# Running the first element's layer 1 by itself inside a third layer 0, with a three-deep ring of score tiles, and a new order of the layers

## The chip, the cores and the metric

The kernel runs on one core of one Trainium2 chip. The metric is device time in microseconds (us) of one launch, smaller is better. The engines are named as in the profile: PE (matrix multiplication), PEld (its weight loads), DVE (vector), ACT (activation functions), POOL, and SP (the queue that issues most DMAs).

## The reference, cut to what matters

Four attention layers follow one another over a tensor of 4 elements of 64 x 64 x 64 (4096 tokens of 64 channels each). The elements are independent.

```
layer 0:  e = softmax(q k^T) over 4096 keys;  out[n] = sum over m of e[m, n] v[m];  x = gamma * out + x
layer 1:  theta = x Wt (8 channels); phi, g = maxpool2(x Wp), maxpool2(x Wg)   (1024 keys, 8 and 32 channels)
          x = x + sigma * (softmax(theta phi^T) g) Wo
layer 2:  group norm (per channel pair), attention over 4096 keys, projection, x = x + ...
layer 3:  group norm, attention over 4096 keys, projection, out = norm(x) + ...
```

Layers 0, 2 and 3 each form 4096 x 4096 scores per element. Layer 1 forms 4096 x 1024, a small part of the work.

## The kernel before

All arithmetic is in float32. A big attention (layer 0, 2 or 3 of one element) is a **stage** of 64 equal **steps**. This text writes L2/0 for the stage "layer 2 of element 0". There are twelve stages; before the change their order is L0/0, L0/1, L2/0, L0/2, L2/1, L0/3, L2/2, L3/0, L3/1, L2/3, L3/2, L3/3.

In a step, `first` makes two score tiles `s` (128 x 1024, two PSUM banks each) with four 64 x 512 matmuls apiece, and ACT writes exp of each into an SBUF tile `p`. The step also issues the second products of an earlier step (`adds` in layer 0, `then` in `attention`): they multiply `p` by the values and sum into accumulators `acc`. In layer 0 these lag three steps, and four accumulators (one bank each) stay open for the whole stage; in layers 2 and 3 they lag two steps and use two accumulators. PSUM has room for two `s` tiles (`ps_s`) and four single banks (`ps_a`); the latter are the accumulators. There are 14 `p` buffers and 13 buffers of 128 x 2048 (`x_p`).

In layers 2 and 3 the row sums are formed by DVE additions of `p` into `zacc` (L1299 in the profile). In layer 0 ACT adds them up as it writes the exponentials (`accum_out`, L1009), except where `back["at"]` is LATE or END: there ACT runs without it (L1006) and DVE reduces the tile (L1007).

Everything else is **background**: layer 1, and the preparation of later stages (`before0`, `before2`, `before3`: transposes, norms, projections, values; `loads`: the input DMA). A background is a Python generator that yields places. `step` advances it at the place MID, between the two second products of the step, and at LATE, inside the second one; an END advances after all the work of the step. `tempo` says how many advances a step earns, and at most one MID and one LATE happen in a step. `urgent` work (closing a chunk of layers 2 and 3) goes ahead of MID. `drain`, after a stage, issues all that the background has left, at once. The program order so made is the order on every engine; nothing is reordered later.

Layer 1 of an element has a prefix (theta, phi, g: L1075, L1092, DMAs that swap halves), 16 **units** (two halves j of the queries by eight blocks k of 128 keys), and `finish`. A unit is `scores` (eight matmuls with 8 rows each into two `s` tiles, L1122; two exponentials, L1128; DVE adds them to `zacc1`, L1137) and, one unit later, `add` (four 128 x 32 matmuls, L1148). For elements 1 to 3 layer 1 runs in the background of a layer 2, which needs only two accumulators, so `add` sums in a bank of its own. For element 0 it runs in the background of L0/1, where all four banks are taken: each `add` writes a fresh `s` tile, and DVE adds it to an SBUF tile (L1157).

The backgrounds before, by stage:

```
L0/0: rest of element 0's preparation, constants, loads(1), before0(1), loads(2)
L0/1: layer 1 of 0, before2(0)          L2/0: layer 1 of 1, before0(2)
L0/2: before2(1), loads(3)              L2/1: layer 1 of 2, before0(3)
L0/3: before2(2)                        L2/2: layer 1 of 3, before3(0)
L3/0: before3(1)    L3/1: before2(3)    L2/3: before3(2)    L3/2: before3(3)    L3/3: -
```

Where a layer 2 follows a layer 0, `not_before` holds the second products of layer 2 back until layer 0's accumulators are released, so that the fourth step of that layer 2 has two steps' worth of them.

Of the kernel before, what the change touches and what calls it, by code (L numbers as in the profile page):

```python
# [11 lines left out]
ALU = mybir.AluOpType  # L12
# [585 lines left out]
def fast_path(tc: tile.TileContext, a: dict, out: bass.AP, bad, read_flag):  # L598
# [18 lines left out]
    D8, D2 = C // 8, C // 2  # L617


    MID, ALONE, LATE, END = range(4)  # L620

    ctx = ExitStack()
    ctx.enter_context(tc.manual_schedule())
# [158 lines left out]
    def background(tempo, *phases):  # L782
# [5 lines left out]
        back.update(gen=pieces(), credit=0.0, tempo=tempo)  # L788
        back["at"] = next(back["gen"], None)

    def drain():
        while back["at"] is not None:
            while urgent:
                urgent.pop(0)[1]()
            back["at"] = next(back["gen"], None)
# [20 lines left out]
    def step(first=None):  # L816
        back["credit"] = min(back["credit"] + back["tempo"], 3.0)
        for f in before.pop(now[0], ()):
            f()
        if first is not None:  # L820
            first()
        work = due.pop(now[0], [])
        for n, f in enumerate(work[:2]):
            if n == 1:
                advance(MID)
            split = n == 1 and ready(LATE)
            f(lambda: advance(LATE)) if split else f()
        for f in work[2:]:
            f()
        if len(work) < 2:  # L830
            advance(MID)
            advance(LATE)
        passes = list(later)
        later.clear()
        for f in passes:
            f()
        advance(END)
        now[0] += 1

    def until(st, *names):  # L840
# [134 lines left out]
            for _ in g:  # L975
                pass

    def layer0(st):

        q, k, v = st.pop("q"), st["x"], st.pop("v")
        pairs = NB * NC // 2
        acc, ps, zs, scaled = {}, {}, {}, {}
        zsum, rz = check_columns(NB)

        def queries(m, i, e):

            c, n = divmod(m // 2, 4)
            return q[(c + i) % 2][half(i), ds(c // 2 * 1024 + m % 2 * 512 + n * P + e * C, C)]  # L990

        def first(u):
            m, c = divmod(u, NC)
            if c == 0:
                zs[m] = small.tile([P, NC], FP, tag="z0", name="z0")
            s = s_tile()
            for i in range(2):
                for e in range(2):
                    nc.tensor.matmul(  # L999
                        s[half(e), chunk(i)], queries(m, i, e), k[half(i), chunk(c)], start=True, stop=True  # L1000
                    )
            p = ps[u] = p_tile()
            z = zs[m][:, c : c + 1]
            if back["at"] in (LATE, END):

                nc.scalar.activation(p, s, AF.Exp)  # L1006
                nc.vector.tensor_reduce(z, p, AX.X, ALU.add)  # L1007
            else:
                nc.scalar.activation(p, s, AF.Exp, accum_out=z)  # L1009
            if c == NC - 1:  # L1010
                nc.vector.tensor_reduce(zsum[:, m : m + 1], zs.pop(m), AX.X, ALU.add)  # L1011
                nc.vector.reciprocal(rz[:, m : m + 1], zsum[:, m : m + 1])

        def scale(t):
            m = 2 * t // NC
            vs = scaled[t] = z_p.tile([P, C], FP, tag="vs", name="vs", bufs=1)
            nc.scalar.activation(vs, v[:, m, :], AF.Copy, scale=rz[:, m : m + 1])  # L1017

        def add(t, e, n, cols):

            m, second = divmod(2 * t, NC)
            c = (second + 2 * e) % NC + n
            if c not in acc:
                acc[c] = acc_tile()
            for i in range(2):
                nc.tensor.matmul(  # L1028
                    acc[c][half(i), cols], scaled[t][half(e), :], ps[NC * m + c][half(e), chunk(i)][:, cols],
                    start=(m == 0 and not second), stop=(m == NB - 1 and second > 0),  # L1030
                )
                yield

        def adds(t, n, within=None):
            for cols in parts(within, t * 2 < NC or t >= pairs - NC // 2):
                for row_tiles in zip(add(t, 0, n, cols), add(t, 1, n, cols)):
                    pass
            if n == 1:
                del scaled[t]
                if t % 2:  # L1040
                    for u in range(2 * t - 2, 2 * t + 2):
                        ps.pop(u)

        def finish(cs):
            xT = st["x"]
            for c in cs:
                nc.vector.scalar_tensor_tensor(xT[:, chunk(c)], acc.pop(c), gamma0, xT[:, chunk(c)], ALU.mult, ALU.add)
            if not acc:
                st["done0"] = True

        start = now[0]
        for t in range(pairs):
            g = start + t + 3
            before.setdefault(g, []).append(lambda t=t: scale(t))
            due.setdefault(g, []).extend([lambda *within, t=t, n=n: adds(t, n, *within) for n in range(2)])
        due[start + pairs + 2].append(lambda: finish((0, 2, 1, 3)))
        for t in range(pairs):
            step(lambda: (first(2 * t), first(2 * t + 1)))
        return start + pairs + 3


    def layer1(on, st, bank):

# [44 lines left out]
        yield from [MID] * 3  # L1110

        ps, accs, zaccs, os = {}, {}, {}, {}

        def scores(j, k):

            ss = [s_tile() for e in range(2)]
            n, d = divmod(k, 2)
            for m in range(2):
                for e in range(2):
                    for i in range(2):  # L1120
                        r = slice((2 * e + i) * 32, (2 * e + i) * 32 + D8)
                        nc.tensor.matmul(  # L1122
                            ss[e][half(m), chunk(i)], pgs[0 if e == d else 1][r, ds(n * P + m * C, C)],
                            th[r, chunk(i ^ j)], start=True, stop=True,
                        )
            ps[j, k] = pk = [p_tile() for e in range(2)]
            for e in range(2):
                nc.scalar.activation(pk[e], ss[e], AF.Exp)  # L1128
            if k == 0:
                return lambda: None  # L1130
            if k == 1:
# [7 lines left out]
            return accumulate  # L1139

        def add(j, k):
            if k == (NK - 1 if bank else 0):
                os[j] = o_tile("o1")
            if k == 0 and bank:
                accs[j] = acc_tile()
            acc = accs[j] if bank else s_tile()[:, 0:512]
            for q in range(4):
                nc.tensor.matmul(  # L1148
                    acc[quarter(q), :], g[:, k, :], ps[j, k][q // 2][:, chunk(q % 2)],
                    start=(k == 0 or not bank), stop=(k == NK - 1 or not bank),  # L1150
                )
            if k > 0:
                del ps[j, k]
            if k == 1:
                del ps[j, 0]
            if not bank and k > 0:
                nc.vector.tensor_tensor(os[j], os[j], acc, ALU.add)  # L1157
            elif not bank or k == NK - 1:
                nc.scalar.copy(os[j], acc)

        def normalise(j):

# [40 lines left out]

        todo = [(j, k) for j in range(2) for k in range(NK)]
        for n in range(len(todo) + 1):
            accumulate = None
            if n < len(todo):
                yield LATE
                accumulate = scores(*todo[n])
            if n:  # L1210
                if not bank:
                    yield END
                elif n == len(todo):
                    yield LATE
                add(*todo[n - 1])
            if accumulate and bank:
                later.append(accumulate)
            elif accumulate:
                accumulate()
        if bank:  # L1220
            for j in range(2):
                yield from finish(j)
        else:
            ends = [finish(j) for j in range(2)]
            at = [next(end) for end in ends]
            while at[0] is not None:
                if at[0] == ALONE:
                    yield ALONE
                    at[0] = next(ends[0], None)
                yield at[1]  # L1230
                at = [at[0] if at[0] != at[1] else next(ends[0], None), next(ends[1], None)]
        st["done1"] = True


# [538 lines left out]
    background(1.0, rest(st0), second_half(s0, s0["v"]), pause(6), constants(), loads(s1), pause(6), before0("DVE", s1), loads(s2))  # L1773
    layer0(s0)
    drain()
    background(3.0, layer1("DVE", s0, False), before2("DVE", s0))
    free = layer0(s1)
    drain()
    background(3.0, layer1("ACT", s1, True), before0("ACT", s2))
    free = layer2(s0, free)  # L1780
    drain()
    background(1.0, before2("DVE", s1), loads(s3))
    free = layer0(s2)
    drain()
    background(3.0, layer1("ACT", s2, True), before0("ACT", s3))
    free = layer2(s1, free)
    drain()
    background(1.0, before2("DVE", s2))
    free = layer0(s3)
    drain()  # L1790
    background(3.0, layer1("ACT", s3, True), before3("ACT", s0))
    free = layer2(s2, free)
    drain()
    background(0.6, before3("ACT", s1))
    free = layer3(s0, free)
    drain()
    background(0.6, before2("ACT", s3))
    free = layer3(s1, free)
# [88 lines left out]
```

## Time and profile before

| | |
|---|---|
| median of 3 runs | 2928.45 us (2926.47 to 2929.64) |
| time of the profiled execution | 2926.57 us |
| its span, first to last instruction | 2924.8 us |
| PE busy | 2893.5 us, 99% |
| DVE busy | 1871.4 us, 64% |
| ACT busy | 1799.6 us, 62% |
| granted TensorE clock, mean | 0.998 |

The rows of the profile name a line of the kernel, an engine, an operation and its tiles (out<-in). Each matmul of the program appears as two MATMUL records, so eight records of 64 x 512 are four matmuls. A busy PE is not a PE at its peak: matmuls are pipelined on parts of the array, and a step that waits a little between its matmuls still shows as busy.

### The profile page before, as it was taken

Reading aid. Unit: us, or ns where it says so; the run is one execution under the profiler, and the core shown is the slowest. Engines: PE = TensorE matmul, PEld = TensorE weight load, DVE = VectorE, ACT = ScalarE, POOL = GpSimd, SP = SyncE. Lnnn points to the kernel's source line nnn. Section 1 sums busy time; section 2 is a strip of 40 time slices with the busy share of each in tenths; the row PEclk is TensorE's granted clock in tenths of the full one; section 3 lists DMA queues with packets and bytes.
Section 4 is the critical chain, followed back from the end, with each engine's and each line's share of the span. In section 5 each row is a group of like instructions: output and inputs, shape, how many; then the busy total and the mean of one; then the engine's idle time right before and its main releaser. Section 6 shows DMA issues by size and latency. Waiting matters only on the chain.

```text
span 2924.8 us, 66545 instructions
## 1 busy us (share of the span) xinstructions
PE 2893.5 (99%) x29397; PEld 1130.5 (39%) x29397; DVE 1871.4 (64%) x2141; ACT 1799.6 (62%) x2481; POOL 33.7 (1%) x33
## 2 busy tenths in 40 slices
PE   9999999999999999999999999999999999999998
PEld 3333233333444433344443343444344444443333
DVE  2111753589821078963027898888888877878878
ACT  5666666665566766566766655555555555555554
POOL 0000000000000000000000000000000000000000
PEclk9999999999999999999999999999999999999999
DMA  2010000000001000000000000000000000000000
GB/s 38 1 30 7 1 1 16 7 5 5 20 5 30 1 7 5 5 23 16 1 1 7 5 9 20 19 5 9 5 19 8 20 5 7 6 20 5 8 5 10
DMA packets 85993, 30.64 MB, mean 10 GB/s; under 512 B 79680, under 2 KB 83776, under 8 KB 84288
## 3 DMA queue, kind: packets, MB, share of 16 engines
q1 hardware_dynamic: 83440, 25.90, 4.8%
q8 instruction: 232, 3.80, 0.6%
q10 hardware_dynamic: 2256, 0.41, 0.1%
q14 instruction: 65, 0.53, 0.1%
HBM read 4.79 MB, written 4.19 MB: 3 GB/s over the span
## 4 chain that ended last, share of the span: by engine, by line
PE 97%; DVE 1%; ACT 1%; issue 0%; DVEq 0%
PE acc L1323 30%; PE s L1288 30%; PE s L999 15%; PE acc L1028 15%; PE s L1122 2%; PE acc L1148 2%; ACT p L1128 1%; DVE zacc L1299 1%; PE s L1148 1%; PE s L891 0%; PE s L1419 0%; PE s L912 0%; PE s L1467 0%; PE s L1194 0%; PE s L1092 0%
## 5 line engine op out<-in xcount | busy, mean ns | idle before, releaser
L1293 ACT ACTIVATE p<-s 128x1024 f32<-128x1024 f32 x1024 | 994.5, 1022 | 694.8 <-PE s L1288 675.1
L1299 DVE TENSOR_TENSOR zacc<-zacc,p 128x1024 f32<-128x1024 f32 x960 | 1174.1, 1223 | 179.7 <-ACT p L1293 114.7
L1323 PE MATMUL acc<-p,v 64*64 64x512 f32 (+1 forms) x8576 | 1007.7, 572 | 0.0
L1009 ACT ACTIVATE p<-s 128x1024 f32<-128x1024 f32 x480 | 486.9, 1020 | 114.8 <-PE s L999 114.7
L1323 PEld LDWEIGHTS acc<-p,v 64*64 64x64 f32 x8576 | 348.7, 133 | 536.7 <-issue 536.7
L1028 PE MATMUL acc<-p,vs 64*64 64x512 f32 (+1 forms) x4224 | 501.4, 577 | 0.0
L1288 PE MATMUL s<-q,k 64*64 64x512 f32 x2048 | 491.5, 590 | 2.1 <-ACT p L1128 2.1
L1288 PE MATMUL s<-q,xT 64*64 64x512 f32 x2048 | 491.3, 590 | 0.0
L999 PE MATMUL s<-xT,q 64*64 64x512 f32 x2048 | 487.3, 591 | 2.4 <-DVE mean L1355 0.7
L999 PE MATMUL s<-xT,q_swapped 64*64 64x512 f32 x2048 | 487.7, 591 | 0.3 <-DVE o L1157 0.3
L1288 PE MATMUL s<-q,h_swapped 64*64 64x512 f32 x2048 | 480.7, 590 | 3.9 <-DVE v L916 3.5
L1288 PE MATMUL s<-q,k_swapped 64*64 64x512 f32 x2048 | 480.4, 590 | 0.0
L1011 DVE TENSOR_REDUCE all_z<-z 128x1 f32<-128x4 f32 x128 | 20.1, 157 | 606.4 <-ACT p L1009 602.7
L1028 PEld LDWEIGHTS acc<-p,vs 64*64 64x64 f32 x4224 | 173.5, 133 | 265.8 <-issue 264.0
L1288 PEld LDWEIGHTS s<-q,h_swapped 64*64 64x64 f32 x2048 | 149.5, 133 | 140.2 <-issue 127.2
L1288 PEld LDWEIGHTS s<-q,xT 64*64 64x64 f32 x2048 | 149.9, 133 | 133.2 <-issue 127.0
L1288 PEld LDWEIGHTS s<-q,k_swapped 64*64 64x64 f32 x2048 | 148.1, 133 | 137.5 <-issue 87.1
L999 PEld LDWEIGHTS s<-xT,q_swapped 64*64 64x64 f32 x2048 | 146.4, 133 | 141.7 <-issue 110.2
L999 PEld LDWEIGHTS s<-xT,q 64*64 64x64 f32 x2048 | 144.3, 133 | 139.2 <-issue 110.8
L1288 PEld LDWEIGHTS s<-q,k 64*64 64x64 f32 x2048 | 148.6, 133 | 116.6 <-issue 96.2
L1017 ACT ACTIVATE vs<-v,all_r 128x64 f32<-128x64 f32 x256 | 89.1, 348 | 157.7 <-PE acc L1028 80.5
L1128 ACT ACTIVATE p<-s 128x1024 f32<-128x1024 f32 x128 | 124.1, 1021 | 82.4 <-PE s L1122 78.5
(212 smaller groups left out, 1318.5 us busy)
## 6 DMA issues: line engine op xcount, KB each, us to landing
k_swapped<-k SPq DMA_DIRECT2D x8, 512.0 KB, 5.4
residual<-turned SPq DMA_DIRECT2D x128, 32.0 KB, 1.8
h_swapped<-xT SPq DMA_DIRECT2D x8, 512.0 KB, 5.3
out_dram<-turned SPq DMA_DIRECT2D x60, 64.0 KB, 2.0
xin<-in_x_dram SPq DMA_DIRECT2D x12, 256.0 KB, 6.4
q_swapped<-q SPq DMA_DIRECT2D x6, 512.0 KB, 5.3
pg<-pg SPq DMA_DIRECT2D x8, 128.0 KB, 2.3
xin<-in_x_dram SPq DMA_DIRECT2D x12, 64.0 KB, 2.3
```

The lines of the kernel that those rows point to most:

```text
L999: nc.tensor.matmul(s[half(e), chunk(i)], queries(m, i, e), k[half(i), chunk(c)], start=True, stop=True)
L1009: nc.scalar.activation(p, s, AF.Exp, accum_out=z)
L1011: nc.vector.tensor_reduce(zsum[:, m : m + 1], zs.pop(m), AX.X, ALU.add)
L1017: nc.scalar.activation(vs, v[:, m, :], AF.Copy, scale=rz[:, m : m + 1])
L1028: nc.tensor.matmul(acc[c][half(i), cols], scaled[t][half(e), :], ps[NC * m + c][half(e), chunk(i)][:, cols], start=(m == 0 and not second) ...
L1122: nc.tensor.matmul(ss[e][half(m), chunk(i)], pgs[0 if e == d else 1][r, ds(n * P + m * C, C)], th[r, chunk(i ^ j)], start=True, stop=True,)
L1128: nc.scalar.activation(pk[e], ss[e], AF.Exp)
L1148: nc.tensor.matmul(acc[quarter(q), :], g[:, k, :], ps[j, k][q // 2][:, chunk(q % 2)], start=(k == 0 or not bank), stop=(k == NK - 1 or not ...
L1288: nc.tensor.matmul(s[half(e), chunk(i)], k[(j + i) % 2][half(i), ds(j // 2 * P + e * C, C)], q[half(i), chunk(c)], start=True, stop=True,)
L1293: nc.scalar.activation(p, s, AF.Exp)
L1299: add = lambda: nc.vector.tensor_tensor(zaccs[c], p0, p, ALU.add)
L1323: nc.tensor.matmul(accs[c][e][half(i), cols], v[half(e), j, :], p[half(e), chunk(i)][:, cols], start=(j == 0), stop=(j == NB - 1),)
```

## The change

- The order of the stages becomes L0/0, L0/1, L0/2, L2/0, L0/3, L2/1, L3/0, L2/2, L3/1, L2/3, L3/2, L3/3.
- Element 0's layer 1 is made with `held=True`. Its prefix runs in the background of L0/1, after `before0` of element 2. It then yields HOLD, where `drain` stops. L0/2 is called with `hold=release`: at its fourth step, before that step's own matmuls, `release` runs all 16 units in one go with nothing between them. At that moment L0/1's four accumulators are released and L0/2 has opened none, so two banks of `ps_a` serve as a third score tile (`slots[2]`), and the other two as the accumulators of the two halves. `slot` hands out two `s` tiles and the pair of banks in turn. An exponential out of the pair of banks is two instructions of 512 columns. After the units, `finish` and `before2` run in the background of L0/2.
- Layer 1's other form, that sums in an SBUF tile, goes, and END with it; `adds` of layer 1 in layer 2 stand at the same places as before.
- Layer 0's exponentials always use `accum_out`.
- The backgrounds move with the stages:

```
L0/1: before0(2), prefix of layer 1 of 0            L0/2: 16 units alone; finish of layer 1 of 0, before2(0)
L2/0: loads(3), layer 1 of 1, before0(3)            L0/3: before2(1)
L2/1: layer 1 of 2, before3(0)                      L3/0: before2(2)
L2/2: layer 1 of 3, before3(1)                      L3/1: before2(3)
L2/3: before3(2)     L3/2: before3(3)     L3/3: -
```

The diff, cut:

```
+    def release():
+        assert back["at"] == HOLD
+        back["at"] = next(back["gen"])
+
     def drain():
-        while back["at"] is not None:
+        while back["at"] not in (None, HOLD):
...
@@ layer0
-            if back["at"] in (LATE, END):
-                nc.scalar.activation(p, s, AF.Exp)
-                nc.vector.tensor_reduce(z, p, AX.X, ALU.add)
-            else:
-                nc.scalar.activation(p, s, AF.Exp, accum_out=z)
+            nc.scalar.activation(p, s, AF.Exp, accum_out=z)
...
         start = now[0]
+        if hold is not None:
+            before.setdefault(start + 3, []).append(hold)
...
@@ layer1
+        slots = [None, None, None]
+        if held:
+            yield HOLD
+            slots[2] = [acc_tile() for i in range(2)]
+        turns = [0]
+
+        def slot():
+            if held:
+                turns[0] += 1
+            own = slots[turns[0] % 3]
+            s = None if own else s_tile()
+            return own or [s[:, chunk(i)] for i in range(2)], s
...
-            ss = [s_tile() for e in range(2)]
+            ss = [slot() for e in range(2)]
...
-                nc.scalar.activation(pk[e], ss[e], AF.Exp)
+                banks, s = ss[e]
+                for dst, src in [(pk[e], s)] if s is not None else [(pk[e][:, chunk(i)], banks[i]) for i in range(2)]:
+                    nc.scalar.activation(dst, src, AF.Exp)
...
         for n in range(len(todo) + 1):
-            accumulate = None
-            if n < len(todo):
+            if not held:
                 yield LATE
-                accumulate = scores(*todo[n])
+            accumulate = scores(*todo[n]) if n < len(todo) else None
             if n:
-                if not bank:
-                    yield END
-                elif n == len(todo):
-                    yield LATE
                 add(*todo[n - 1])
-            if accumulate and bank:
-                later.append(accumulate)
-            elif accumulate:
-                accumulate()
+            if accumulate:
+                accumulate() if held else later.append(accumulate)
...
-    background(3.0, layer1("DVE", s0, False), before2("DVE", s0))
+    background(1.0, rest(before0("DVE", s2)), layer1("DVE", s0, held=True), before2("DVE", s0))
     free = layer0(s1)
     drain()
-    background(3.0, layer1("ACT", s1, True), before0("ACT", s2))
+    back["tempo"] = 3.0
+    free = layer0(s2, hold=release)
+    drain()
+    background(3.0, loads(s3), layer1("ACT", s1), before0("ACT", s3))
     free = layer2(s0, free)
...
```

## The prediction

> **What bounds the kernel now.** I read the page first, then the busy time of each stage, then the timeline inside the stages that cost most.
>
> ```profile
> span 2924.8 us, 66545 instructions
> PE 2893.5 (99%) x29397; PEld 1130.5 (39%) x29397; DVE 1871.4 (64%) x2141; ACT 1799.6 (62%) x2481; POOL 33.7 (1%) x33
> ...
> PE 97%; DVE 1%; ACT 1%; issue 0%; DVEq 0%
> ```
>
> The chain that ended last runs through PE for 97% of the span. So a change gains only by giving PE fewer matmuls or by making it wait less. Matmuls stay the same in number, so the waits decide, and the page hides them: a stretched step counts as busy.
>
> They show in the length of a step, from one step's first exponential to the next one's on ACT. In the timeline an undisturbed step takes 3.43 us everywhere, 64 of them 219.6 us. What a stage takes beyond that is its background and its waits. The windows of four stages (length first, then busy time by engine, the granted clock, DMA):
>
> ```profile
> 248.26:528.17 279.91, 270.38 (x2804) 92.56 (x2800) 133.38 (x198) 185.51 (x323) 5.43 (x1) 1.00 0.03 7
> 796.91:1022.36 225.45, 224.72 (x2220) 95.25 (x2216) 38.48 (x106) 157.72 (x320) 5.43 (x1) 1.00 0.07 12
> 1516.54:1785.53 268.99, 268.22 (x2888) 100.05 (x2880) 227.19 (x223) 163.96 (x174) 1.46 (x1) 1.00 0.04 10
> 1785.53:2015.18 229.65, 226.17 (x2260) 95.08 (x2264) 187.34 (x183) 131.12 (x138) 1.46 (x1) 0.99 0.05 11
> ```
>
> These are L0/1, L0/2, L2/2 and L3/0; over 219.6 they have 60.3, 5.8, 49.4 and 10.0 us. L0/1, the stage the change takes apart, is the dearest of all twelve. Its units run from the step at 285.49 to the one at 396.37: 18 steps in 110.88 us, that is 49.1 above 18 x 3.43. One of these steps in the timeline (start, duration):
>
> ```profile
> 303.97 1.94 ACT L1006 ACTIVATE p<-s 128x1024 f32<-128x1024 f32 x2 [1.06 <-PE s L999]
> ...
> 304.60 1.47 PE L1028 MATMUL acc<-p,vs 64*64 64x512 f32 x16
> ...
> 306.00 1.11 PE L1122 MATMUL s<-th,pg 8*64 8x512 f32 x16
> 307.05 0.66 PE L1028 MATMUL acc<-p,vs 64*64 64x256 f32 x8
> 307.19 1.94 ACT L1128 ACTIVATE p<-s 128x1024 f32<-128x1024 f32 x2 [1.28 <-PE s L1122]
> ...
> 308.27 1.06 PE L1148 MATMUL s<-p,pg 128*32 128x512 f32 x8 [0.56 <-ACT p L1128]
> ```
>
> It takes 6.45 us, 3.02 more than a plain step, though its unit holds only 2.04 us of PE work (scores 306.00 to 307.05; add 308.27 to 309.26, where the next stage matmul starts). The other microsecond is the ring of two score tiles: scores wait for the stage's exponentials, the add needs a score tile as well and waits for the unit's first exponential, the next `first` waits for the second and for DVE.
>
> The chip also loses a visible piece at the start of L3/0. In the waits of PE:
>
> ```profile
> PE s L1288 <- DVE v L916: 3.5, 1, 3.5
> ```
>
> This is `drain` at the end of L2/2: both value tiles of before3(0) are issued in the last step, both score tiles wait for DVE (whose queue holds two 1.27 us additions and a 1.25 us transpose), and L3/0's first step takes 8.60 us.
>
> **The units alone (L0/2, fourth step).** Count from T, when PE could go on with the stage. Ready: at the same seam between L0/0 and L0/1 the last second products start at 255.74, T is 257.46, and DVE's four updates (L1047, 2.73 us together) start at 256.85. So the first two of the four banks are free at T + 0.8; in the built order these are the two that become the third tile. The first unit's scores end at T + 1.9, its first exponential starts at T + 2.0.
>
> Period: in the built order of the changed kernel the first tile of unit n needs the exponential 2n-3, the second the exponential 2n-2. So one exponential of the pair is always under way while PE works. From the end of exponential 2n-2: scores after 0.09 (305.91 to 306.00), the next exponential 1.19 after them (306.00 to 307.19), and 1.02 for itself: 2.30 us. In the 1.28 of that ACT does the pair's other exponential (0.92 when back to back, half of 1.94). Five of the 16 first tiles are the pair of banks, two exponentials of 512: the nearest row, L1159's copy of 512, takes 585 ns against L878's 1016 for 1024, so 1.08 to 1.17 instead of 1.02; I take 1.08. Fifteen periods: 15 x 2.30 + 5 x 0.06 = 34.8, and 0.2 for the one ACT copy between the halves. DVE needs 14 x 2.35 = 32.9 (303.55 in the timeline: two additions in 2.35), PE 16 x 2.04 = 32.6: both just under it, and `p` buffers are reused only four units later. So the last pair starts at T + 37.0, ends 2.0 later, the last add takes 0.9 more: **39.9 us** for what now costs 49.1. Bounds: PE alone, 2.0 + 32.6 + 1.9 = 36.5; both exponentials waited for, a period of 1.28 + 1.94 = 3.22, 2.0 + 15 x 3.22 + 2.9 = 53.2. The value is nearest to the first, since the built order shows which exponential is waited for.
>
> Behind this block wait: on PE the rest of L0/2 (that is the 39.9), on ACT the next `vs` scaling, on DVE layer 0's sums of 0.16 us. The six `p` tiles of steps one to three are ready when it ends. SP issues nothing in it.
>
> **The rest of layer 1 and before2(0).** `finish` cost 2.7 in L0/1 (both halves interleaved); apart, as in L2/0, two L1194 of 0.86 and two sums of 0.3: 2.3. The prefix (2.9) and before2(0) (5.5) only change stage. Layer 0's sums on ACT again (198 ns each, 32 of them) lie in ACT's idle time: a plain step there uses 2.6 of 3.43.
>
> **Moved backgrounds.** I price each stage by the one that has the same work now, in us above 219.6:
>
> - L0/1: 60.3 now. Then before0(2) 3.8 (in L2/0, the five steps from 741.24) and the prefix 2.9: 6.7.
> - L0/2: 5.8 now. Then 39.9 + 2.3 + 5.5 = 47.7.
> - The three layers 2 with a layer 1: 49.1, 49.1, 49.4 now. Then before0 sits in one and before3 in two: 49.1 + 49.4 + 49.4, less 1.7, since L2/2 now follows a layer 3 and has no step with doubled second products (5.15 us at 538.47): 146.2 after 147.6.
> - L0/3: 5.8 both times (before2).
> - L3/0: 10.0 now. Then before2, as in L3/1 now (6.8), and 0.3 for the end of a layer 2 before it: 7.1.
> - L3/1: 6.8 now, then 7.1. The others keep their work.
>
> The stall of 5.2 is inside the 10.0. It goes because these layers 1 no longer wait for their layer 0 to end: in the built order before3(0)'s value tiles come in the 60th and 61st step of L2/1 instead of both in the last. Those of before3(1) come in the last two steps of L2/2, one each, as the 53rd and 54th of L2/0 have them now at 0.97 a piece. loads(3) goes ahead of layer 1's DMAs on SP, in L2/0's first step; the first wait for those is six steps later.
>
> Sum: before 60.3 + 5.8 + 147.6 + 5.8 + 10.0 + 6.8 = 236.3; after 6.7 + 47.7 + 146.2 + 5.8 + 7.1 + 7.1 = 220.6: **15.7 us less**. The profiled execution took 2926.57, so 2910.9. The median of before is 1.9 higher; by it, 2912.8. I say 2912.
>
> **A rule against it.** The windows of the granted clock: 1.00 from 285.49 to 396.37, though PE shows 9.2 us of idle time in these 110.88; but
>
> ```profile
> 1784.00:1791.00 7.00, 3.46 (x63) 1.37 (x57) 5.94 (x6) 1.02 (x1) 0.00 (x0) 0.82 0.01 2
> ```
>
> around the 3.5 us stall, after which 64 x 512 matmuls take 1.12 us instead of 0.59. So the clock falls after a long wait, and short ones, 0.4 to 0.6 apiece, left it alone. The new block's waits are of the short kind, about 0.3 us per unit and 0.9 at its ends, so I price no loss.
>
> [...]
>
> **The rivals.**
>
> 1. *The third tile does not decouple* (same). Each unit waits for both its exponentials: the block takes 53.2, the gain is 2.4, 2926. For it: scores of both tiles are interleaved, so the first cannot finish alone. Against: the waits in the built order.
> 2. *The clock falls in the block* (slower). At the 1.06 us that those slowed matmuls settle at, for 0.59, a unit needs 2.04 x 1.80 = 3.67 on PE, the block 2.0 + 58.7 + 2.9 = 63.6: 8.0 us slower, 2936. It decides from a block of 55.6 us, 3.4 a unit. Against: 1.00 in the units of now.
> 3. *The stall only moves* to L3/1: 5.2 back, 2917. For: value tiles still stand in L2/2's last two steps. Against: one a step, and DVE's additions of that step are issued after it.
>
> That the change does not do what it says is excluded by the built order: the 16 units stand alone, with the banks as every third tile.
>
> **How the numbers follow.** Forecast 0.78; third tile 0.08; clock 0.06; moved stall 0.08. Range: down by 3.4 (block at 36.5), 2 for the median against one execution and 2.6 for stages priced by another's row: 2904. Up by the moved stall and by a block midway to rival 1 with the same 2: about 2922. Left out: rivals 1 and 2 and a little, under 2 in 10. A measurement can tell about 0.2%, 5.9 us. Faster 0.86, same 0.08, slower 0.06.
>
> **What would show it.** L0/2 of about 267 us, L0/1 of 226; in the block exponentials about 2.3 us a unit, clock 1.00; L3/0's first step 3.43; no wait of PE for L916's line over 1 us. A block over 46 us, or another stage 3 us off its price, makes the prediction wrong.

## The result, and the profile after

| | before (same chip) | after |
|---|---|---|
| median | 2926.51 us (2924.86 to 2929.64) | 2937.46 us (2936.71 to 2938.21) |
| span of the profiled execution | 2924.8 us | 2935.6 us |
| granted clock, mean | 0.998 | 0.989 |

The ratio is 1.0035 [1.0024, 1.0046]: the changed kernel is slower, by about 11 us. The prediction said 2912 and 2904 to 2922; it was wrong, on the other side of no change.

From the page of the changed kernel: span, busy time by engine, the granted clock in 40 slices, and the shares of the chain that ended last.

```profile
span 2935.6 us, 66287 instructions
...
PE 2913.2 (99%) x29269; PEld 1132.9 (39%) x29269; DVE 1826.2 (62%) x2095; ACT 1805.5 (62%) x2524; POOL 33.8 (1%) x33
...
PEclk9999998799999999999999999999999999999999
...
PE 96%; DVE 3%; issue 1%; ACT 0%; DMA 0%; DVEq 0%; ACTq 0%
```

PE is busy for 19.7 us more than before although it has 128 fewer matmul records. That is the first sign that matmuls became slower and not that waits were added. The second is the clock row: an 8 and a 7 in the slices from 440 to 587 us, which lie in L0/2.

The stages of the changed kernel, cut as in the prediction (length, then busy time by engine, granted clock, DMA). These are L0/1, L0/2, L2/0, L2/1, L3/0 and L2/2:

```profile
247.62:473.83 226.21, 226.21 (x2228) 81.46 (x2224) 24.79 (x78) 157.95 (x320) 0.00 (x0) 1.00 0.04 8
473.83:763.05 289.22, 288.24 (x2644) 98.21 (x2640) 85.16 (x148) 190.65 (x365) 5.43 (x1) 0.90 0.06 9
763.05:1033.94 270.89, 268.58 (x2876) 104.49 (x2872) 225.89 (x210) 161.87 (x170) 0.00 (x0) 1.00 0.04 10
1259.39:1530.23 270.84, 269.01 (x2892) 102.52 (x2888) 228.94 (x224) 164.18 (x175) 1.46 (x1) 1.00 0.04 10
1530.23:1757.06 226.83, 226.59 (x2260) 97.32 (x2256) 195.30 (x194) 128.69 (x135) 5.44 (x1) 1.00 0.05 11
1757.06:2025.49 268.43, 267.19 (x2884) 97.00 (x2880) 231.70 (x230) 163.89 (x174) 1.46 (x1) 1.00 0.05 11
```

| stage | priced | measured |
|---|---|---|
| L0/1 | 226.3 | 226.2 |
| L0/2 | 267.3 | 289.2 |
| three layers 2 with a layer 1, above 3 x 219.6 | 146.2 | 151.4 |
| L3/0 (first step 3.43 both) | 226.7 | 226.8 |
| L3/1 | 226.7 | 226.8 |

Two rows are off. L0/2 has 21.9 us too much, the three layers 2 have 5.2. With the 15.7 that was priced as gain, 21.9 + 5.2 - 15.7 = 11.4, and the span grew by 10.8.

In L0/2 all of it is in the block: the step that holds the 16 units takes 65.25 us, so the block is 65.25 - 3.43 = 61.8 against 39.9 priced. Windows of the changed kernel in and around the block:

```profile
476.00:485.00 9.00, 9.00 (x88) 2.92 (x80) 2.90 (x6) 4.93 (x10) 0.00 (x0) 1.00 0.01 2
485.00:486.00 1.00, 0.12 (x2) 0.00 (x0) 0.15 (x1) 0.98 (x2) 0.00 (x0) 1.00 0.00 0
486.00:487.00 1.00, 0.90 (x6) 0.32 (x12) 0.00 (x0) 1.00 (x3) 0.00 (x0) 0.57 0.00 0
495.00:505.00 10.00, 10.00 (x64) 1.27 (x56) 5.60 (x6) 5.50 (x8) 0.00 (x0) 0.50 0.01 2
545.00:555.00 10.00, 10.00 (x96) 3.52 (x93) 2.71 (x5) 7.79 (x16) 0.00 (x0) 1.00 0.00 0
```

The first unit's scores run at 1.00. At 486.13 the granted clock goes to 0.50, and it stays there until 544.16, while the block's last two adds follow one another (from 541.32); the stage's own matmuls start only at 544.80. In the window from 495 the profile has PE busy for all of its 10.00 us: this is no stall, it is work at half speed. ACT, which should have been near its limit, is busy for 5.50. A unit in the timeline (start, duration):

```profile
495.64 1.94 PE L1160 MATMUL acc<-p,pg 128*32 128x512 f32 x8
495.79 1.02 ACT L1143 ACTIVATE p<-s 128x1024 f32<-128x1024 f32 x1 [1.82 <-PE acc L1135]
496.71 1.08 ACT L1143 ACTIVATE p<-acc 128x512 f32<-128x512 f32 x2
497.51 2.01 PE L1135 MATMUL s<-th,pg 8*64 8x512 f32 x16
499.45 1.94 PE L1160 MATMUL acc<-p,pg 128*32 128x512 f32 x8
499.59 1.94 ACT L1143 ACTIVATE p<-s 128x1024 f32<-128x1024 f32 x2 [1.81 <-PE s L1135]
```

Scores take 2.01 us where the rows of before had 1.11, the add 1.94 where they had 1.06; the period is 3.80 us (495.79 to 499.59), PE's alone, and ACT waits 1.8 us for PE in each. The two exponentials of 512 take 1.08 together, as priced.

### The profile page after: what moved, and what is told of

It is laid out like the page before. It is cut to its first block, busy times and chain, and to the rows that moved or that the text cites. A ratio compares the mean times of both kernels' runs of the same rounds, so it can differ in the third digit from the quotient of the medians.

```text
span 2935.6 us, 66287 instructions
## 1 busy us (share of the span) xinstructions
PE 2913.2 (99%) x29269; PEld 1132.9 (39%) x29269; DVE 1826.2 (62%) x2095; ACT 1805.5 (62%) x2524; POOL 33.8 (1%) x33
## 4 chain that ended last, share of the span: by engine, by line
PE 96%; DVE 3%; issue 1%; ACT 0%; DMA 0%; DVEq 0%; ACTq 0%
PE acc L1317 29%; PE s L1282 29%; PE s L1002 15%; PE acc L1026 15%; PE acc L1160 3%; PE s L1135 2%; DVE zacc L1293 2%; PE s L915 0%; PE s L894 0%; PE s L1413 0%; PE acc L1135 0%; ACT p L1143 0%; PE s L1092 0%; PE s L1205 0%; PE s L1461 0%
## 5 line engine op out<-in xcount | busy, mean ns | idle before, releaser
L1287 ACT ACTIVATE p<-s 128x1024 f32<-128x1024 f32 x1024 | 994.9, 1022 | 693.7 <-PE s L1282 668.2
L1007 ACT ACTIVATE p<-s 128x1024 f32<-128x1024 f32 x512 | 519.7, 1020 | 118.3 <-PE s L1002 118.2
L1026 PE MATMUL acc<-p,vs 64*64 64x512 f32 x4096 | 496.7, 590 | 0.0
L1026 PEld LDWEIGHTS acc<-p,vs 64*64 64x64 f32 x4096 | 165.0, 133 | 260.5 <-issue 259.1
L1143 ACT ACTIVATE p<-s 128x1024 f32<-128x1024 f32 x117 | 114.1, 1022 | 81.4 <-PE s L1135 69.4
```

The source lines that it names most:

```text
L1026: nc.tensor.matmul(acc[c][half(i), cols], scaled[t][half(e), :], ps[NC * m + c][half(e), chunk(i)][:, cols], start=(m == 0 and not second) ...
L1143: nc.scalar.activation(dst, src, AF.Exp)
```

## The experiments

Four theories stood against each other. *Rows*: the clock falls because the scores read 8 of the 32 rows of each of the four groups of `theta`. *Pauses*: it falls because PE is idle for a moment in every unit. After the first four runs came *onset*, that only the first 3 us or the first wait of the block decide, and *latch*, that a fallen clock stays down until the stage's matmuls return. What is left at the end is called *share* here: the clock goes by how much of the array is at work over some microseconds. It is a reading of mine that the outcomes fit; no run shows it by itself. `r` is the slice of rows that a score matmul reads; the rows after the first 8 of each group of `theta` are zeros, so that a wider slice adds nothing to the sums.

### All 32 rows in the block

```
-  r = slice((2*e+i)*32, (2*e+i)*32 + D8)
+  r = slice((2*e+i)*32, (2*e+i)*32 + (32 if held else D8))
```

> The score matmuls of the 16 units in the block take 32 rows instead of 8; the 24 added rows of theta are zeros, so the sums stay and no instruction is added. In the changed kernel the block takes 61.8 us at a granted clock of 0.50. Theory 'rows' (the clock falls because too few rows of the array work in the scores, 8 of each 32, although PE is never idle): clock 1.00 in the block, block about 40 us, time 21 to 22 us below the changed kernel, that is 10 to 12 below the kernel before. Rival 'pauses' (the clock falls because PE waits a little in every unit): nothing changes, block 61.8 at 0.50. Rival 'seam' (the two waits of 0.9 and 1.0 us at the block's start drop the clock, and what follows only cannot raise it): the clock falls for some us at the start, and whether 32 rows raise it again is open: a block of 40 to 62.

Measured: 2914.47 us (2913.97 to 2914.85), ratio to before 0.9957 [0.9943, 0.9971]. Its window over most of the block, and two rows of its timeline:

```profile
483.00:521.00 38.00, 36.90 (x385) 9.31 (x382) 32.73 (x31) 32.14 (x44) 0.00 (x0) 1.00 0.01 2
```

```profile
499.55 1.29 PE L1135 MATMUL s<-th,pg 32*64 32x512 f32 x16
500.77 1.07 PE L1160 MATMUL acc<-p,pg 128*32 128x512 f32 x8
```

The clock is 1.00, and the add, which was not edited, is back at 1.07. The block's step takes 42.34 us, the block 38.9 (39.9 were priced), L0/2 266.3. So the 23 us between this kernel and the changed one are the clock's, and multiplying zeros brings them back. What makes the clock fall is not settled by it: the rows were changed, but with the speed the waits changed too.

### The same with two score tiles

```
-  own = slots[turns[0] % 3]
+  own = None                       (and the 32 rows)
```

> As e1_rows32, but without the pair of banks as a third score tile: the units use the two score tiles alone. If the clock stays at 1.00, each unit waits for both exponentials of the one before, 3.22 us a unit, and the block takes about 53 us instead of 40: 13 us slower than e1_rows32. If the third tile decouples nothing, the same time as e1_rows32. If the clock falls here, about 62 or more.

Measured: 2927.25 us, ratio 1.000 [0.9991, 1.001]; the block is 51.7 us at clock 1.00. Two exponentials of its timeline:

```profile
499.69 1.94 ACT L1143 ACTIVATE p<-s 128x1024 f32<-128x1024 f32 x2 [1.27 <-PE s L1135]
502.84 1.94 ACT L1143 ACTIVATE p<-s 128x1024 f32<-128x1024 f32 x2 [1.21 <-PE s L1135]
```

A unit takes 3.15 us: 1.94 for both exponentials and 1.21 of waiting for PE, which itself waits for both. The third tile is worth 51.7 - 38.9 = 12.8 us; the prediction's two prices, 53.2 and 39.9, differ by 13.3. Also, the whole gain over before hangs on the third tile.

### The 8-row scores twice, and once with 32 and once with 8 rows

```
-  for m in range(2): ...
+  for rr in ([D8, D8] if held else [D8]):         first kernel
+  for rr in ([32, D8] if held else [D8]):         second kernel
+      for m in range(2): ...                      (slice of rr rows; the second pass writes the same sums again)
```

> The changed kernel with each score matmul of the block issued twice in a row into the same place (8 rows, the second overwrites the first with the same values). At full clock a unit then needs about 3.0 us of PE, more than ACT and DVE, so that PE does not pause in the block. 'Pauses': the clock stays at 1.00 and the block takes about 52 us, 10 less than in the changed kernel although it has more work. 'Rows': the clock falls to 0.50 all the same, a unit needs about 5.9 us and the block about 97. 'Seam': as 'rows'.

> The counterpart of e3_twice8 with as many instructions: each score matmul of the block is issued with 32 rows and then with 8 into the same place, the sums being the same. Theory 'share' (the gate weighs how much of the array works, over some three microseconds, and rows that take no part count as idle; PE's pauses matter only as a part of that): clock 1.00 all through, about 3.0 us a unit on PE, block about 50 instead of e3_twice8's 87. Rival: it is the doubled matmuls, or 8 rows wherever they stand, that drop the clock: 0.50 and 85 or more.

Measured: 2963.34 us (one run) and 2927.82 us (one run). The instructions are the same in number, order and shape of output; only the rows of half the scores differ. The windows of the first and of the second:

```profile
491.00:565.00 74.00, 74.00 (x540) 14.61 (x544) 30.55 (x26) 27.05 (x37) 0.00 (x0) 0.50 0.00 1
```

```profile
484.00:530.00 46.00, 44.98 (x589) 16.85 (x577) 29.40 (x26) 28.92 (x40) 0.00 (x0) 1.00 0.01 2
```

In the first the profile has no idle moment of PE in 74 us, and the granted clock is 0.50. So no pauses are needed to keep the clock down, and *pauses* falls as the reason for the 0.50 in the units. In the second PE does pause, for 1.02 us in the block's opening, and the clock is 1.00. The opening of the first has the same wait, 1.03 us, and its clock falls at 488.92, 1.4 us after it: that few rows alone, without a pause, would make the clock fall is not shown. Blocks: 87.5 us (97 was expected by *rows*) and 52.6 us (50). The "three microseconds" over which *share* was to count is an estimate that no run shows; in the changed kernel 2.99 us lie between the block's first scores (483.14) and the fall (486.13).

### 32 rows in the first six units only

```
+  ... + (32 if held and (j, k) < (0, 6) else D8)
```

> The changed kernel with 32 rows in the scores of the first six units only, 8 rows in the other ten. 'Rows': clock 1.00 in the first six units (2.3 us each), 0.50 some us after them (3.8 us each): the block about 55. 'Seam': if 32 rows carry the block over its start, the clock stays at 1.00 to the end, block about 40. 'Pauses': 0.50 from the start, block 61.8.

Measured: 2915.62 us (one run), block 38.9, as with 32 rows throughout. The window of the six units, then that of the ten with 8 rows:

```profile
484.00:498.00 14.00, 13.02 (x143) 3.36 (x142) 10.84 (x12) 10.82 (x15) 0.00 (x0) 1.00 0.01 1
498.00:521.00 23.00, 22.88 (x242) 5.79 (x244) 20.89 (x20) 20.62 (x29) 0.00 (x0) 1.00 0.01 2
```

Ten 8-row units in 23 us leave the clock at 1.00. So *rows* falls in its plain form, that 8-row units cannot hold the clock. Here they held it, at full speed already. It also shows that 32 rows cost no more time here than 8: the block's step is 42.34 us in both, and a score matmul record takes 613 ns in the mean in both, first with 32 rows throughout (486 to 521), then with 8 in the ten units:

```profile
L1135 PE MATMUL s<-th,pg 32*64 32x512 f32 x156 | 18.6, 613 | 1.0 <-ACT p L1143 1.0
```

```profile
L1135 PE MATMUL s<-th,pg 8*64 8x512 f32 x104 | 12.7, 613 | 0.0
```

### 32 rows in the first unit only, and no first wait

```
+  ... + (32 if held and (j, k) == (0, 0) else D8)      first kernel
-  turns = [0]                                          second kernel (8 rows)
+  turns = [-1]
```

With `turns` at -1 the first unit takes two `s` tiles and the second unit starts on the free pair of banks, so the wait of 1.0 us before the second unit's scores goes.

> The changed kernel with 32 rows in the scores of the first unit only, 8 rows in the other fifteen. Theory 'onset' (the clock is dropped by the first three microseconds of the block alone, which hold 8-row scores and two waits and no add yet; later units, each with a full add, keep a full clock but cannot win it back): clock 1.00, block 39 as in e1_rows32, 23 us below the changed kernel. Theory 'rows' in a weaker form (several units of 8 rows have to follow one another early): the clock falls after the first unit, block 55 to 60.

> The changed kernel with 8 rows throughout, but the two score tiles handed out first and the pair of banks third (turns from -1): the first unit does not wait 0.4 to 0.9 us for layer 0's last updates on DVE. One of the block's two opening waits is gone, the other, for the first exponential, stays at about 1 us or grows to 1.3. If the clock needs both waits to fall, it stays at 1.00 and the block takes about 38. If the 8-row scores with one wait are enough, it falls to 0.50 and the block takes about 61.

Measured: 2936.61 and 2936.46 us (one run each), blocks of 60.5 and 61.1. The window of the first in which its clock falls:

```profile
486.00:489.40 3.40, 2.56 (x28) 0.89 (x36) 0.34 (x1) 3.17 (x5) 0.00 (x0) 0.96 0.00 0
490.00:540.00 50.00, 50.00 (x326) 6.92 (x312) 29.46 (x26) 26.25 (x36) 0.00 (x0) 0.50 0.01 1
```

With 32 rows in the first unit the fall comes one unit later, at 489.15 for 486.13, and the clock stays down. Without the first wait, of which 0.33 us are left, it comes at 486.81. Neither the first 3 us nor the first wait decides alone; *onset* falls in that form.

### 16 rows throughout, and 32 rows from the seventh unit

```
+  ... + (16 if held else D8)                            first kernel
+  ... + (32 if held and (j, k) >= (0, 6) else D8)       second kernel
```

> The changed kernel with 16 rows in all scores of the block, between the 8 that lose the clock and the 32 that keep it. 'Share': 16 rows give the opening about half of what 32 give it, and the outcome is open: if the clock holds, the block takes 39 and the kernel some 22 us less than the changed one; if it falls, the steady units, with more of the array at work than in the changed kernel, may win it back after some units: 39 to 62.

> The changed kernel with 8 rows in the first six units and 32 in the other ten. The clock falls at the start as in the changed kernel, and a unit takes 3.8 us. 'Share': with 32 rows PE uses nearly all it can at half clock, so the clock comes back within a few us of the seventh unit and the rest takes 2.3 us a unit: block about 48. 'Latch' (once down, only the stage's own matmuls bring it back): 0.50 to the end, block about 62.

Measured: 2935.46 us with 16 rows (one run), block 60.3: the clock falls and does not come back.

```profile
490.00:540.00 50.00, 50.00 (x328) 6.95 (x312) 29.06 (x26) 26.25 (x36) 0.00 (x0) 0.50 0.01 1
```

With 32 rows from the seventh unit: 2922.75 us (one run), block 47.2. Its windows from just before the first 32-row scores, which start at 504.78:

```profile
504.00:507.00 3.00, 3.00 (x24) 0.53 (x24) 2.36 (x2) 1.24 (x3) 0.00 (x0) 0.50 0.00 0
507.00:510.00 3.00, 3.00 (x32) 0.39 (x24) 2.08 (x2) 2.57 (x4) 0.00 (x0) 0.91 0.00 0
510.00:522.00 12.00, 12.00 (x134) 3.29 (x136) 9.69 (x10) 10.96 (x16) 0.00 (x0) 1.00 0.01 2
```

The clock is back at 507.56, 2.8 us after the first 32-row scores, in the middle of the block and with PE as busy as before it (3.00 of 3.00 us). *Latch* falls: with the rows given, and nothing else changed, the clock came back. A return within a few microseconds, while PE's busy share stays the same, is what *share* asks for.

### The new order without the block

Layer 1 of element 0 in its old form, in the background of L0/2, with the change's order of stages.

```
-  background(1.0, rest(before0("DVE", s2)), layer1("DVE", s0, held=True), before2("DVE", s0))
+  background(1.0, rest(before0("DVE", s2)))
...
-  free = layer0(s2, hold=release)
+  background(3.0, layer1("DVE", s0, False), before2("DVE", s0))
+  free = layer0(s2)
```

> The new order of the stages alone: element 0's layer 1 in its old form (sums in SBUF through score tiles, units between the second products), in the background of L0/2 with before2(0), and before0(2) in L0/1. By the prediction's table the order is worth 15.7 - 9.2 - 0.4 = 6 us. By the stages measured in the changed kernel (the three layers 2 with a layer 1 at 151.2 over 219.6 instead of 146.2) it is worth 1 us: no difference from before. L0/2 about 280 us, L3/0 about 227 without a long first step.

Measured: 2925.56 us (2924.09 to 2927.29), ratio 0.9996 [0.9987, 1.0005]: no change that can be told. L3/0 is 226.82, so the stall is gone as priced; L2/0 and L2/1 take 270.78 and 270.89, so they have the excess of the changed kernel too. It belongs to the order, not to the clock.

### A later start for two backgrounds

```
-  background(3.0, loads(s3), layer1("ACT", s1), before0("ACT", s3))
+  background(3.0, loads(s3), pause(2), layer1("ACT", s1), before0("ACT", s3))
...
-  background(3.0, layer1("ACT", s2), before3("ACT", s0))
+  background(3.0, pause(3), layer1("ACT", s2), before3("ACT", s0))      (and the 32 rows)
```

> e1_rows32 with layer 1 of elements 1 and 2 started two and three steps later in their layer 2 (pause(2), pause(3)), so that the sums of finish no longer fall on the step after the closing of a chunk of that layer 2 (steps 40 and 41, or 39 to 41, of the changed kernel). If that collision is what makes L2/0 and L2/1 270.8 us instead of the 269 they were priced at, L2/0 and L2/1 come down by 1.5 to 2 us each and the kernel is 3 to 4 us faster than e1_rows32, about 0.6% faster than before. If not, the same as e1_rows32.

Measured: 2912.11 us (2910.58 to 2912.35), ratio 0.9946 [0.9933, 0.996]. L2/0 is 269.08 and L2/1 270.07, against 270.84 and 270.81 with 32 rows alone. 1.8 and 0.7 us come back of the 5.2; 3 to 4 were expected. The meeting described below is gone with the shift: PE's wait for L1467, 2.2 us with 32 rows alone, is no longer among its waits, and the steps 39 to 41 come down by 2.0 us in L2/0 and by 1.7 in L2/1. In L2/1 other steps take 1.0 of that back.

### All together

32 rows, both later starts, and `turns = [-1]`.

> e8_rows32_pause with the two score tiles handed out first and the pair of banks third (turns from -1), so that the block's first unit does not wait for layer 0's last updates. With 32 rows in all units the clock stays at 1.00; the block is 0.5 to 1 us shorter than e8_rows32_pause's 38.9, and the kernel 0.5 us faster than it: some 15 us below the kernel before and 25 below the changed one.

Measured: 2911.93 us (2911.67 to 2912.29), ratio to before 0.995 [0.9936, 0.9963]; block 38.2. It is the same as the one before it within the runs' scatter, and it beats the kernel before by 0.5% and the changed one by 0.9%.

## Why the prediction was wrong, point by point

**The step that failed** is the one under "A rule against it": "The new block's waits are of the short kind, about 0.3 us per unit and 0.9 at its ends, so I price no loss." I read the clock by PE's idle time. The twice-8 kernel shows no idle time in 74 us of its block and runs at 0.50 there. In the L0/1 of before the same 8-row units stood among the stage's 64-row matmuls, and its clock of 1.00 spoke for that mixture, not for the units alone. Taking the units out of the mixture is what the change does, so this row could not speak for the block. By *share*, what was to be counted is how much of the array works in a few microseconds; an estimate of it stands below.

**The second rival** is what happened, and its price held: block 63.6 priced, 61.8 measured; 2936 priced, 2937.46 measured. It decided from 3.4 us a unit; 3.8 were seen. Its chance of 0.06 was the mistake, not its sum, though that the total comes so near is partly luck: the block was 1.8 us shorter than priced there, and the three layers 2, which it did not doubt, 5.2 us longer.

**The third tile** decouples as said: 38.9 us at full clock for 39.9 priced, 12.8 us less than with two tiles for 13.3. The first rival falls.

**The stall** of L2/2's end went and did not come again: L3/0's first step is 3.43, L3/1 within 0.1 us of its price. The third rival falls.

**The moved backgrounds** were right for L0/1, L3/0 and L3/1 and mis-sized for the layers 2: 146.2 priced, 151.4 measured (51.3, 51.2 and 48.8). I priced each by the stage with the same work and did not ask at which step two pieces would meet. The waits of PE in the changed kernel name such a meeting in L2/0 and L2/1:

```profile
PE s L1282 <- DVE xT L1467: 2.3, 2, 1.6
```

L1467 is DVE's last operation in closing a chunk of layer 2. It reads an `s` tile, and `finish`'s sums (L1187) take the other one for DVE a step later. In L2/0 the 41st step is 5.53 us long, and in L2/1 the 39th to 41st take 3.71, 4.44 and 4.42 instead of 3.43. The 1.1 us of L2/2, and what the shifted starts left in L2/1, are not traced to a cause. So the order alone, priced at 6.1 us (15.7 less the block's 9.2 and `finish`'s 0.4), brought 1.7 by medians of the same chip (2927.26 to 2925.56), which the interval given above does not tell from nothing, and most of the rest was given back in these stages.

**The sum corrected.** The order 1.7 us faster, the block with its third tile at full clock 11 faster (2914.47 for 2925.56), the clock 23 slower (2937.46 for 2914.47): with these three, taken on chips whose runs of the kernel before agree within 1 us, one comes out at 10 us slower. They divide the difference that was measured and are no check of it. The forecast's 2912 was meant for a kernel that keeps its clock: with that alone restored, by the 32 rows, the time is 2914.47. The 2911.93 of the last run came from two more edits, so that it meets the forecast is luck.

**When the clock changed.** The experiments leave open why ten 8-row units hold 1.00 after six full units and not after one. The traces say when the clock changed. These are the stretches at 0.50, from fall to return, first in the kernel before, around its stall of 3.54 us at L3/0:

```profile
1788.44:1791.85 3.41, 2.84 (x16) 1.02 (x20) 1.64 (x2) 0.79 (x1) 0.00 (x0) 0.50 0.00 0
```

Then in the changed kernel, with 32 rows in the first unit, with 32 rows from the seventh, and with the 8-row scores twice:

```profile
486.13:544.16 58.03, 58.03 (x363) 8.48 (x364) 32.33 (x28) 31.08 (x43) 0.00 (x0) 0.50 0.00 1
```

```profile
489.15:543.76 54.61, 54.61 (x344) 7.88 (x340) 32.67 (x28) 29.04 (x40) 0.00 (x0) 0.50 0.00 1
```

```profile
487.08:507.56 20.48, 20.48 (x130) 2.87 (x128) 11.80 (x10) 10.80 (x15) 0.00 (x0) 0.50 0.00 1
```

```profile
488.92:570.84 81.92, 81.92 (x588) 15.80 (x576) 33.05 (x28) 30.20 (x41) 0.00 (x0) 0.50 0.01 1
```

The four are within 0.03 of 17, 16, 6 and 24 times the 3.41 us of the first. This is arithmetic on five measured lengths; what sets the lengths is not shown.

What follows is an estimate from the matmul records: rows times columns of each record, weighted by the columns of data that it streams (512 for most), summed and set against a plain step of 3.43 us as 1.00. A plain step has 32 records of 64 x 64, of 0.59 us each, which overlap. A unit has 16 of 8 x 64 and 8 of 128 x 32, which is 0.31 of a plain step. A unit of the twice-8 kernel has 0.38, in about 5.4 us (544 weight loads in 74 us, 40 to a unit). Beside each estimate stands the clock that the trace has there.

| a unit, estimated | at full clock, in 2.3 us | at half clock, in 3.8 us (twice-8: 5.4) |
|---|---|---|
| scores with 8 rows | 0.47: stayed at 1.00 for ten units, 23 us | 0.28: stayed at 0.50, 58.03 us |
| with 8 rows, twice | not run | 0.24: stayed at 0.50, 81.92 us |
| with 16 rows | 0.56: not run | 0.34: stayed at 0.50, 50 us of window |
| with 32 rows | 0.75: stayed at 1.00, 38 us of window | 0.45: back at 1.00 after 2.8 us |

So the estimate puts the units of these runs in the order of their outcomes. Busy time does not: the twice-8 kernel is busy throughout (74.00 of 74.00 us). Nor does counting each group of 32 rows as full where 8 are read: then a unit of the twice-8 kernel counts 0.48 and stays at 0.50, and one with 32 rows counts 0.45 and comes back.

The loss began in the block's opening, where a wait of PE stands beside scores with one add at most. The 3.41 us before the fall, as long as the shortest stretch, are estimated in the same way at 0.19 in the changed kernel, with 0.98 us of waiting, and at 0.30 with 32 rows in the first unit only, with 0.99. From there the runs part by the clock the units started at: 8-row units at full clock kept it in the one (1.00 for 23 us), and at half clock the same units did not win it back in the other (0.50 for 58.03 us).

**What stays open.** How small a share makes the clock fall, how large a one brings it back and over what time it counts, if it is the share, is not shown: the estimate counts the records that the trace has, and no run varied the share finely. In each fall in the block the microseconds before it hold a pause of PE, of 0.33 us at the least, so a fall by few rows alone is not shown. Most variants ran once, so those with few 32-row scores, in the first unit only or before the 8-row ones, might come out otherwise in another run.

## What to carry to other kernels

When matmuls that use few rows are taken out of a dense stream and run by themselves, do not read their clock from the mixed stream (1.00 in L0/1 of before, 0.50 in the block here), nor from how busy PE is (10.00 of 10.00 us at 0.50). Estimate how much of the array works over a few microseconds, the count that put these runs in order, and look first at the opening, where waits stand beside them (0.98 us here). If the tile has room for rows of zeros, try them: reading them cost no time here (613 ns a score record with 32 rows and with 8) and the clock stayed at 1.00. When backgrounds move to other stages, price not only their work but the step at which they meet the stage's own closing work, above all where both borrow a score tile.

## What the runs showed of the hardware that was not expected

- A PE that was busy for 74.00 of 74.00 us was granted half its clock when the matmuls between the full adds used 8 of 32 rows; with half of them at 32 rows as many instructions got 1.00. With 16 rows throughout the block it was 0.50 (490 to 540 us), with 32 it was 1.00 (483 to 521 us).
- The clock that 8-row units did not win back (0.50 for 58.03 us) they kept elsewhere: 1.00 for the 23 us of ten such units after six with 32 rows.
- The added rows of `theta` are zeros, and with them the block had 1.00 in place of 0.50 all the same.
- The stretches at 0.50 lasted 3.41 us in the kernel before, 58.03 in the changed one, and 20.48, 54.61 and 81.92 in three variants. With 32-row scores from 504.78 the clock was back at 507.56, without a pause and without other work.
- The number of rows did not change the time of a score matmul at full clock: 613 ns in the mean for a record with 32 rows and with 8.
